# Graph attention: weighted rows in a tile of their own, carried counts taken from the destinations, the carried row read ahead of the copy, and two quads' logits in one PSUM bank

## The chip, the cores and the metric

The kernel runs on one core of a Trainium2 chip. The metric is the device time of one execution in microseconds (us), lower being better; it is stated as the median of several runs. PE is the tensor engine (PEld its weight loads), DVE the vector engine, ACT the scalar engine, POOL the GpSimd engine, and SP the engine that here only issues DMAs.

## What is computed

A residual layer of graph attention over 12,500 nodes of 128 values and 200,000 edges, sorted by destination, with 64 values per edge and 4 heads of 32:

```python
h = jnp.maximum(_layernorm(x, axis=-1), 0.0)
# _L0_gnn_ref(h, (src, dst), edge_attr_64, W_node, W_edge, a):
h = (node_features @ W_node.T).reshape(num_nodes, H, HD)
e = (edge_features @ W_edge.T).reshape(num_edges, H, HD)
att = jnp.sum(jnp.concatenate([h[src], h[tgt], e], axis=-1) * a, axis=-1)
att = jnp.where(att > 0, att, 0.2 * att)
m = jnp.maximum(jax.ops.segment_max(att, tgt, num_segments=num_nodes), 0.0)
ex = jnp.exp(att - m[tgt])
deg = jax.ops.segment_sum(ones, tgt, num_segments=num_nodes)
denom = segment_sum(ex, tgt) + (num_edges - deg)[:, None] * jnp.exp(-m)
w = ex / denom[tgt]
h_prime = segment_sum(w[:, :, None] * h[src], tgt)
# result: x + h_prime
```

## The kernel before

**Tiling.** Edges are cut into 392 groups of 511, each held as 4 chunks of 128 lanes (J = 4); lane 0 of a group is free for a row carried over from the group before, since a destination's edges can run across the boundary. Four groups are a quad (98 quads), and 2 to 4 quads are a super (28 of them), the unit of the softmax. A group's destinations lie within a window of 96 nodes (WIN).

**Prologue.** x is loaded, normalized and multiplied with the weights, and one row of 137 values per node goes to a table in HBM: 4 heads of 32 values and a one (132), a count (R_CNT), and 4 source logits (R_SRC). For the first four quads POOL gathers raw rows of x instead, which need no table (64 gathers from the start on). `indexed` derives the per-group tables from the destinations: the first node of each window (`base`), the lane's slot in the window, `is_last` (the lane's destination is the group's last one), and `cont` and `thru` (the group goes on with the destination before; it holds only that one).

**Main loop.** The order is written out by hand: `together` takes steps in turn from generators, so that in program order a group of `sums(q)`, a group of `all_logits` of a later quad and a step of `softmax(s)` alternate. Each engine runs its own instructions in that order, and waits on semaphores that other engines and DMAs raise.

- `fetch(q + 2)`, called when the logits of quad q open, issues the edge features and destinations (L283, L285), the windows (one TensorLoad of a register per group, L458), four small DMAs for target logits (`pw`, L468) and four for x (`xw`, L470) on SP, and 16 indirect gathers on POOL (L137), one for each chunk of 128 rows. The gathered rows go to `ga`, a ring of eight quads.
- `logits(q, i)` compares destinations (DVE, L500) and multiplies on PE (L505, L508) into `lg`. `flush` adds the pieces up (L520) and the source logits from `ga` (L522) into `U`.
- `softmax(s)` turns U over (L548), takes the slope (ACT L550, DVE L553), scans for the maximum over each destination (L557, L582, L584), and leaves in PSUM the exponentials `ex`, with the factors `facs` of the carried row and the maxima `xs` copied out (L607, L612).
- `sums(q)` writes the maxima over the source logits in `ga` (ACT, L680), multiplies the gathered values by `ex` in place (DVE, L687), builds the marks `hot` (DVE, L691) and sums the rows on PE: three matmuls for chunks 1 to 3 (L696), and a stop matmul for chunk 0 (L639), which waits for the carried row. `complete` runs one group late: it multiplies the carried row out of the PSUM `acc` of the group before (DVE, L634), copies the carried count (ACT, L638, one element), issues the stop matmul, and copies `acc` out to `pt` (ACT, L640). The matmuls are in float32 and appear as two each in the profile.
- After the last group of a quad, `divide` (L708 to L722) makes the result, and SP writes it with one DMA per group (L724), each after a register load of its own (L458).

The carried row of a group thus passes from PE (L639) over ACT (L640), DVE (L634) and ACT (L638) back to PE: L634 is placed behind L640, which reads the same `acc`. A slot of the ring `ga` is free once L639 of its group has read it.

## Time and profile before

| what | before |
|---|---|
| median of 3 runs | 2578.58 us (2570.87 to 2586.93) |
| profiled execution, its own time | 2600.19 us |
| its span | 2598.4 us |
| mean granted clock of PE | 0.536 of full speed |
| PE / PEld / DVE / ACT / POOL busy | 54 / 48 / 53 / 16 / 58% |
| HBM traffic | 114 GB/s over the span |
| stage of the gathers from the table | about 294 to 2473 us |

The profile is one execution on the chip, so sums over its instructions are to be held against its own 2600.19 us. A line number such as L639 is that of the kernel's source. An idle time is followed by what ended it; "issue" means that nothing in the profile held the engine, and "remote" that the event which ended the wait is not in the record.

### The profile page before, as it was taken

What the parts mean: (1) busy time and instruction counts of PE and PEld (TensorE: products, weight loads), DVE (VectorE), ACT (ScalarE), POOL (GpSimd) and SP (SyncE); (2) the same over time, 40 slices, a digit from 0 to 9 for tenths busy, and PEclk for the clock granted to TensorE, in tenths of its full rate; (3) what the DMA queues carried; (4) which work ended last, traced back from release to release, by engine and by line L of the source; (5) the groups of instructions that cost most, each with busy time, mean ns of one, the idle gap of its engine ahead of it and who ended that gap; (6) DMA issues with size and microseconds to landing.
All of it is one profiled execution on the core that took longest, in us unless ns stands there. A gap on an engine that the chain in (4) does not pass through costs nothing. (4 is left out here: it accounts for less than half of the span.)

```text
span 2598.4 us, 29393 instructions
## 1 busy us (share of the span) xinstructions
PE 1405.4 (54%) x7275; PEld 1256.7 (48%) x7275; DVE 1367.0 (53%) x3291; ACT 421.7 (16%) x1806; POOL 1508.0 (58%) x1609
## 2 busy tenths in 40 slices
PE   2442665555555555556555555655555555545485
PEld 1331655545545445445445544545544554444375
DVE  2441465555555545555554554654554554555486
ACT  1431411111111111111111111111111111111122
POOL 7235256666666666666666666666666666666603
PEclk9975655555555555555555555555555555555555
DMA  4342455544544454554455445454544544434430
GB/s 150 102 126 53 108 136 124 127 116 118 128 123 113 115 142 107 127 125 117 119 124 124 116 119 123 120 125 117 125 115 118 125 121 116 121 97 112 103 92 17
DMA packets 214495, 299.12 MB, mean 115 GB/s; under 512 B 86121, under 2 KB 162153, under 8 KB 204914
## 3 DMA queue, kind: packets, MB, share of 16 engines
q1 hardware_dynamic: 162512, 184.97, 26.6%
q0 software_dynamic: 50112, 109.65, 19.3%
q10 hardware_dynamic: 1698, 2.58, 0.3%
q8 instruction: 61, 1.00, 0.2%
q14 instruction: 112, 0.92, 0.1%
HBM read 270.49 MB, written 26.52 MB: 114 GB/s over the span
## 5 line engine op out<-in xcount | busy, mean ns | idle before, releaser
L137 POOL DMA_INDIRECT ga<-table,srci x1502 | 1426.7, 950 | 963.2 <-issue 406.0
L696 PE MATMUL acc<-ga,hot 128*97 128x137 f32 x2352 | 649.6, 448 | 341.3 <-ACT ga L680 225.1
L696 PEld LDWEIGHTS acc<-ga,hot 128*97 128x97 f32 x2352 | 518.2, 279 | 366.1 <-ACT ga L680 229.2
L634 DVE TENSOR_TENSOR ga<-acc,facs 1x132 f32<-1x132 f32 x391 | 115.9, 296 | 625.9 <-ACT pt L640 502.1
L639 PE MATMUL acc<-ga,hot 128*97 128x137 f32 x784 | 267.4, 444 | 289.0 <-ACT ga L638 215.5
L508 PE MATMUL lg<-wblk,ea 128*128 128x8 f32 x1568 | 410.5, 360 | 0.0
L508 PEld LDWEIGHTS lg<-wblk,ea 128*128 128x128 f32 x1568 | 383.3, 310 | 0.0
L505 PEld LDWEIGHTS <-at 96*128 96x128 bf16 x1568 | 219.7, 167 | 298.7 <-DVE at L500 115.0
L639 PEld LDWEIGHTS acc<-ga,hot 128*97 128x97 f32 x784 | 190.3, 279 | 320.3 <-ACT ga L638 235.8
L640 ACT COPY pt<-acc 97x137 f32<-97x137 f32 x392 | 107.4, 274 | 1431.8 <-remote 850.5
L505 PE MATMUL lg<-pw,at 96*128 96x12 bf16 x1568 | 170.7, 182 | 239.1 <-DVE at L500 101.2
L687 DVE TENSOR_TENSOR ga<-ga,ex_ps 128x528 f32<-128x528 f32 x392 | 270.0, 689 | 8.4 <-remote 8.0
L500 DVE TENSOR_TENSOR at<-const_ps,db 96x512 bf16<-96x512 f32 x392 | 267.1, 683 | 9.0 <-DMA db<-in_dst_dram 3.2
L691 DVE TENSOR_TENSOR hot<-const_ps,slot 128x384 f32<-128x384 f32 x384 | 209.4, 545 | 0.0
L520 DVE TENSOR_REDUCE st<-lg 128x64 f32<-128x192 f32 x98 | 35.0, 358 | 139.1 <-remote 109.7
L638 ACT COPY ga<-acc 1x1 f32<-1x1 f32 x391 | 59.9, 153 | 228.8 <-DVE ga L634 114.1
L375 PE MATMUL row_ps<-wcat,hT 128*128 128x137 f32 x198 | 40.3, 354 | 79.9 <-DVE hT L367 32.0
L600 PE MATMUL ex_ps<-ident,ex 64*128 64x64 f32 (+2 forms) x112 | 18.6, 315 | 115.6 <-ACT ex L589 49.7
L375 PEld LDWEIGHTS row_ps<-wcat,hT 128*128 128x128 f32 x198 | 34.0, 246 | 86.1 <-issue 46.0
L553 DVE TENSOR_TENSOR t_ps<-t_ps,low 64x511 f32<-64x511 f32 (+2 forms) x28 | 19.2, 687 | 104.4 <-issue 60.2
L137 POOL DMA_INDIRECT ga<-in_x_dram,srci x64 | 60.6, 947 | 20.9 <-issue 19.2
L600 PEld LDWEIGHTS ex_ps<-ident,ex 64*128 64x128 f32 (+2 forms) x112 | 13.8, 208 | 118.3 <-ACT ex L589 51.1
(131 smaller groups left out, 1131.1 us busy)
## 6 DMA issues: line engine op xcount, KB each, us to landing
db<-in_dst_dram SPq DMA_DIRECT2D x98, 768.0 KB
ea<-in_edge_t_dram SPq DMA_DIRECT2D x98, 512.0 KB
ga<-table,srci POOLq DMA_INDIRECT x1502
xw<-in_x_dram SPq DMA_DIRECT2D x392, 48.0 KB
out_dram<-res SPq DMA_DIRECT2D x392, 48.0 KB
pw<-side SPq DMA_DIRECT2D x392, 2.2 KB
table<-row SPq DMA_DIRECT2D x9, 616.5 KB
xt<-in_x_dram SPq DMA_DIRECT2D x9, 576.0 KB
```

Source lines behind the costliest of these rows:

```text
L137: nc.gpsimd.indirect_dma_start(out=ga[:, i, j, 0:width], out_offset=None, in_=rows, in_offset=bass.IndirectOffsetOnAxis(ap=srci[:, g0 + i, ...
L375: nc.tensor.matmul(row_ps[:, t, :ROW], hT[:, t, :], wcat, start=True, stop=True)
L500: nc.vector.tensor_tensor(at[:, i, :], node_ps[0:WIN, g0 + i:g0 + i + 1].to_broadcast([WIN, GE]), db[:, i, :], op=OP.is_equal)
L505: nc.tensor.matmul(lg[:, i, j].rearrange("p k h -> p (k h)"), at[:, i, j * P:(j + 1) * P], sw, start=i + j == 0, stop=False, skip_group_ch ...
L508: nc.tensor.matmul(lg[:, i, 2 * w:2 * w + 2, 0, :], ea[:, i, w, :], wblk, start=False, stop=True, skip_group_check=True)
L634: nc.vector.tensor_tensor(ga[0:1, i, 0, 0:H * HW].rearrange("p (h w) -> p h w", w=HW), before[WIN:WIN + 1, 0:H * HW].rearrange("p (h w) -> ...
L638: nc.scalar.copy(ga[0:1, i, 0, R_CNT:R_CNT + 1], before[WIN:WIN + 1, R_CNT:R_CNT + 1])
L639: nc.tensor.matmul(acc, hot[:, i, 0, :], ga[:, i, 0, :], start=False, stop=True)
L640: nc.scalar.copy(pt[:, i, :], acc)
L687: nc.vector.tensor_tensor(val, val, heads(ex)[:, :, :, g - s0].unsqueeze(3).to_broadcast([P, J, H, HW]), op=OP.mult)
L691: nc.vector.tensor_tensor(hot[:, i, :, 0:WIN], lane_ps.unsqueeze(1).to_broadcast([P, J, WIN]), slot[:, g, :].unsqueeze(2).to_broadcast([P, ...
L696: nc.tensor.matmul(acc, hot[:, i, j, :], ga[:, i, j, :], start=j == 1, stop=False)
```

## The change

- The product of gathered rows and exponentials goes to a new tile `gw` (two groups per buffer, two buffers) rather than back to `ga`. The maxima, with a leading column of ones that takes the place of the count, are copied into it once per pair of groups. The ring slot is thereby free once the multiply has read it.
- The counts carried into each group are computed once, in `indexed`: a matmul of ones with `is_last` (four, accumulated) and a scan over the groups into `came`. The per-group copy L638 goes, and so does the column of ones for the raw quads.
- The carried row is multiplied out of `acc` before `acc` is copied to `pt`; the copy and the exponential behind it move to a function `copied`, issued after the next group's stop matmul, and `divide` comes one `complete` later.
- The logits of two quads share one PSUM tile, and `flush` comes after the first group of the next quad's logits.
- The slope is applied to U in SBUF by one DVE operation; L550 and L553 go. `facs` is copied on one partition by DVE.
- The registers of a quad's windows are loaded by one multi-register load.
- The marks of the last two quads are made one quad ahead each, `hot` has two buffers rather than three, and a check at the end shares tiles with the softmax.

```diff
@@ -114,6 +114,9 @@
     base = consts.tile([1, G], I32, name="base")
     cont = consts.tile([1, G], F32, name="cont")
     thru = consts.tile([1, G], F32, name="thru")
+    came = consts.tile([1, G + 1], F32, name="came")
     flag = consts.tile([1, 1], I32, name="flag")
     quads = blocks(G, QG)
@@ -265,7 +268,6 @@
             nc.scalar.copy(
                 rows[:, :, 0:H * HW].rearrange("p t (h w) -> p t h w", w=HW)[:, :, :, HD],
                 ones[:, 0:1].unsqueeze(2).to_broadcast([P, m * J, H]))
-            nc.scalar.copy(rows[:, :, R_CNT], ones[:, 0:m * J])
             yield
@@ -325,6 +327,15 @@
                                         wide_ps[1].unsqueeze(2).to_broadcast([P, G, J]),
                                         op=OP.is_equal)
                 yield
+                ones_b = index.tile([P, 1], BF16, name="ones_b")
+                nc.vector.memset(ones_b, 1.0)
+                own_ps = wide_ps[0][0:1, :]
+                for j in range(J):
+                    nc.tensor.matmul(own_ps, ones_b, is_last[:, :, j], start=j == 0, stop=j == J - 1)
+                nc.vector.memset(came[:, 0:1], 0.0)
+                yield
+                nc.vector.tensor_tensor_scan(came[:, 1:G + 1], thru, own_ps, initial=0.0,
+                                             op0=OP.mult, op1=OP.add)
                 nc.vector.tensor_scalar(slot[0:1, :, 0], cont, -1.0, None, op0=OP.add)
@@ -444,8 +455,14 @@
         const_ps = ps.tile([P, WIN + G + QG * H], F32, name="const_ps")
         lane_ps, node_ps = const_ps[:, 0:WIN], const_ps[:, WIN:WIN + G]
         share_ps = const_ps[0:WIN, WIN + G:].rearrange("p (g h) -> p g h", h=H)
+        lg_all = ps.tile([P, 2, QG, J, PIECES, H], F32, name="lg")
         nc.vector.tensor_copy(lane_ps, lane)
         nc.vector.tensor_copy(node_ps, node_at)
+        xs_all = consts.tile([P, 2, J, 1 + H, SBG], F32, name="xs_all")
+        nc.vector.memset(xs_all[:, :, :, 0, :], 1.0)
         tops = consts.tile([1, H, len(supers) + 1], F32, name="tops")
         nc.vector.memset(tops, 0.0)
@@ -454,16 +471,18 @@
             g0 = quads[q0][0]
             return g0, quads[q0 + m - 1][0] + quads[q0 + m - 1][1] - g0
-        def window(g):
-            return nc.values_load(
-                base[0:1, g:g + 1], engines=[mybir.EngineType.SP], min_val=0, max_val=N - 1,
-                skip_runtime_bounds_check_because="a destination, which is a node")
+        def windows(q, lo=0, hi=QG):
+            g0, m = quads[q]
+            g0, m = g0 + lo, min(hi, m) - lo
+            return nc.values_load_multi_w_load_instructions(
+                base[0:1, g0:g0 + m], engines=[mybir.EngineType.SP], min_val=0, max_val=N - 1,
+                skip_runtime_bounds_check_because="a destination, which is a node")[1]
         def fetch_windows(q):
             g0, m = quads[q]
             pw = PW[q] = load.tile([WIN, QG, SIDE], BF16, name="pw")
             xw = XW[q] = work.tile([WIN, QG, D], F32, name="xw", bufs=8)
-            at = [window(g0 + i) for i in range(m)]
+            at = windows(q)
             for i in range(m):
                 nc.sync.dma_start(pw[:, i, :], side[bass.ds(at[i], WIN), :])
             for i in range(m):
@@ -488,7 +507,7 @@
             if q + 2 < nq:
                 fetch(q + 2)
             AT[q] = work.tile([WIN, QG, GE], BF16, name="at")
-            LG[q] = ps.tile([P, QG, J, PIECES, H], F32, name="lg")
+            LG[q] = lg_all[:, q % 2]
         def logits(q, i):
@@ -543,14 +562,14 @@
             same, same_next = kp[:R, 1:GE], kp[:R, 2:GE + 1]
             flush()
             u = U.pop(s)
+            nc.vector.scalar_tensor_tensor(u[:, :, :R], u[:, :, :R], SLOPE, u[:, :, :R],
+                                           op0=OP.mult, op1=OP.max)
             t_ps = ps.tile([SBG * H, GE], F32, name="t_ps")
             for j in range(J):
                 nc.tensor.transpose(t_ps[:R, j * P:(j + 1) * P], u[:, j, :R], ident)
             low = turned.tile([P, NE], F32, name="low")
-            nc.scalar.mul(low[:R], t_ps[:R, 1:GE], SLOPE)
             yield
             att = t_ps[:R, 1:GE]
-            nc.vector.tensor_tensor(att, att, low[:R], op=OP.max)
             run = turned.tile([SBG * H, GE], F32, name="run")
             nc.vector.memset(run[:R, 0:1], 0.0)
             run_e = run[:R, 1:GE]
@@ -583,7 +602,7 @@
             top = att
             nc.vector.tensor_tensor_scan(top[:, ::-1], same_next[:, ::-1], att[:, ::-1],
                                          initial=0.0, op0=OP.mult, op1=OP.max)
-            ex = turned.tile([SBG * H, GE], F32, name="ex")
+            ex = turned.tile([P, GE], F32, name="ex")
             nc.vector.memset(ex[:R, 0:1], 0.0)
             nc.vector.tensor_tensor(ex[:R, 1:GE], low[:R], top, op=OP.subtract)
             nc.scalar.activation(ex[:R, 1:GE], ex[:R, 1:GE], AF.Exp)
@@ -604,49 +623,55 @@
             fac_ps = other[:, 0:R]
             nc.tensor.matmul(fac_ps, ones[:R, :], diag[:R, :R], start=True, stop=True)
             facs = turned.tile([P, SBG * H], F32, name="facs", bufs=2)
-            nc.scalar.copy(facs[:, :R], fac_ps)
+            nc.vector.tensor_copy(facs[WIN:WIN + 1, :R], fac_ps[WIN:WIN + 1, :])
             top_ps = other[:, 512 - J * SBG * H:].rearrange("p (j r) -> p j r", j=J)[:, :, 0:R]
             for j in range(J):
                 nc.tensor.transpose(top_ps[:, j, :], run[:R, j * P:(j + 1) * P], ident[:R, :R])
-            xs = turned.tile([P, J, SBG * H], F32, name="xs", bufs=2)
-            nc.scalar.copy(xs[:, :, 0:R], top_ps)
+            xs = xs_all[:, s % 2]
+            nc.scalar.copy(xs[:, :, 1:, 0:m], top_ps.rearrange("p j (h g) -> p j h g", h=H))
+            nc.scalar.copy(xs[0:1, 0, 0, 0:m], came[:, g0:g0 + m])
             XS[s] = ex_ps[:, 0:J * SBG * H].rearrange("p (j r) -> p j r", j=J), xs, facs
             yield
-        begun = []
+        begun, divisions = [], []
         state = {}
         def complete():
-            division = state.pop("division", None)
+            due = [d for d in divisions if d[0] >= nq - 2 or d[-1] == 1]
+            divisions[:] = [d[:-1] + (1,) for d in divisions if d not in due]
+            full = state.pop("full", None)
             if begun:
                 complete_group(*begun.pop())
-            if division:
-                divide(*division)
-
-        def complete_group(q, i, ga, hot, pt, acc, fc):
-            g0, m = quads[q]
-            g = g0 + i
-            if g:
+            if full:
+                copied(*full)
+            for d in due:
+                divide(*d[:-1])
+        def complete_group(q, i, gw, hot, pt, acc, fc):
+            if quads[q][0] + i:
                 before = state["before"]
                 nc.vector.tensor_tensor(
-                    ga[0:1, i, 0, 0:H * HW].rearrange("p (h w) -> p h w", w=HW),
+                    gw[0:1, 0, 0:H * HW].rearrange("p (h w) -> p h w", w=HW),
                     before[WIN:WIN + 1, 0:H * HW].rearrange("p (h w) -> p h w", w=HW),
                     fc.unsqueeze(2).to_broadcast([1, H, HW]), op=OP.mult)
-                nc.scalar.copy(ga[0:1, i, 0, R_CNT:R_CNT + 1], before[WIN:WIN + 1, R_CNT:R_CNT + 1])
-            nc.tensor.matmul(acc, hot[:, i, 0, :], ga[:, i, 0, :], start=False, stop=True)
+            nc.tensor.matmul(acc, hot[:, i, 0, :], gw[:, 0, :], start=False, stop=True)
+            state["before"] = acc
+            state["full"] = q, i, pt, acc
+        def copied(q, i, pt, acc):
             nc.scalar.copy(pt[:, i, :], acc)
-            state["before"] = acc
             part = 1 if q == nq - 1 else 2 if q == nq - 2 else QG
-            if (i + 1) % part == 0 or i == m - 1:
+            if (i + 1) % part == 0 or i == quads[q][1] - 1:
                 lo = i - i % part
                 den = work.tile([WIN, QG, H], F32, name="den")
                 nc.scalar.activation(den[:, lo:i + 1, :], pt[0:WIN, lo:i + 1, R_SRC:R_SRC + H],
                                      AF.Exp, scale=-1.0)
-                state["division"] = q, pt, den, lo, i + 1
+                divisions.append((q, pt, den, lo, i + 1, 2))
@@ -656,7 +681,7 @@
         def marks(q):
             g0, m = quads[q]
-            hot = work.tile([P, QG, J, WIN + 1], F32, name="hot", bufs=3)
+            hot = work.tile([P, QG, J, WIN + 1], F32, name="hot")
             nc.scalar.copy(hot[:, :m, :, WIN], is_last[:, g0:g0 + m, :])
             if q >= nq - FREE:
                 for i in range(m):
@@ -677,15 +702,21 @@
             pt = work.tile([WIN + 1, QG, ROW], F32, name="pt", bufs=3)
             hot = HOT.pop(q) if q in HOT else marks(q)
             for i in range(m):
-                nc.scalar.copy(ga[:, i, :, R_SRC:R_SRC + H], heads(xs)[:, :, :, g0 - s0 + i])
-            for i in range(m):
                 g = g0 + i
-                if q == nq - 1 - FREE and i == 1:
-                    for k in range(FREE):
-                        HOT[nq - FREE + k] = marks(nq - FREE + k)
-                val = ga[:, i, :, 0:H * HW].rearrange("p j (h w) -> p j h w", w=HW)
+                if i == 1 and nq > q + 1 >= nq - FREE:
+                    HOT[q + 1] = marks(q + 1)
+                if i % 2 == 0:
+                    gw2 = work.tile([P, 2, J, ROW], F32, name="gw")
+                    n = min(2, m - i)
+                    nc.scalar.copy(
+                        gw2[:, 0:n, :, R_CNT:R_SRC + H],
+                        xs[:, :, :, g - s0:g - s0 + n].rearrange("p j h g -> p g j h"))
+                gw = gw2[:, i % 2]
+                by_head = lambda t: t[:, :, 0:H * HW].rearrange("p j (h w) -> p j h w", w=HW)
                 nc.vector.tensor_tensor(
-                    val, val, heads(ex)[:, :, :, g - s0].unsqueeze(3).to_broadcast([P, J, H, HW]),
+                    by_head(gw), by_head(ga[:, i]),
+                    heads(ex)[:, :, :, g - s0].unsqueeze(3).to_broadcast([P, J, H, HW]),
                     op=OP.mult)
                 if q < nq - FREE:
                     nc.vector.tensor_tensor(
@@ -693,9 +724,9 @@
                         slot[:, g, :].unsqueeze(2).to_broadcast([P, J, WIN]), op=OP.is_equal)
                 acc = ps.tile([P, 512], F32, name="acc", bufs=3)[0:WIN + 1, 0:ROW]
                 for j in range(1, J):
-                    nc.tensor.matmul(acc, hot[:, i, j, :], ga[:, i, j, :], start=j == 1, stop=False)
+                    nc.tensor.matmul(acc, hot[:, i, j, :], gw[:, j, :], start=j == 1, stop=False)
                 complete()
-                begun.append((q, i, ga, hot, pt, acc, fc[:, :, g - s0]))
+                begun.append((q, i, gw, hot, pt, acc, fc[:, :, g - s0]))
                 yield
         def divide(q, pt, den, lo, hi):
@@ -720,13 +751,16 @@
                 share_ps[:, :n, :].unsqueeze(3).to_broadcast([WIN, n, H, HD]), op=OP.mult)
             add = nc.gpsimd if nq - 1 > q >= nq - 1 - FREE else nc.vector
             add.tensor_tensor(res[:, :n, :], res[:, :n, :], xw, op=OP.add)
+            at = windows(q, lo, hi)
             for i in range(n):
-                nc.sync.dma_start(out[bass.ds(window(quads[q][0] + lo + i), WIN), :], res[:, i, :])
+                nc.sync.dma_start(out[bass.ds(at[i], WIN), :], res[:, i, :])
         def all_logits(q):
+            open_logits(q)
+            logits(q, 0)
+            yield
             flush()
-            open_logits(q)
-            for i in range(QG):
+            for i in range(1, QG):
                 logits(q, i)
                 yield
             state["logits"] = q
...
@@ -810,11 +843,12 @@
                     together(all_logits(a))
                 if not s:
                     complete()
+                    complete()
                     together(*late(3))
             flush()
             together(sums(nq - 1))
-            complete()
-            complete()
+            for _ in range(3):
+                complete()
             together(check_steps)
             redo = nc.values_load(flag[0:1, 0:1], min_val=0, max_val=1)
```

More of the change, by code (lines that the diff above doesn't have):

```diff
@@ L764, in checked @@
             for k, (g0, n) in enumerate(blocks(G, P)):
-                rows = turned.tile([P, NE + 1], I32, name="rows")
+                rows = turned.tile([P, GE], F32, name="ex").bitcast(I32)
                 nc.scalar.dma_start(rows[:n], dst_rows[g0:g0 + n, 0:NE + 1])
-                yield
                 falls = turned.tile([P, NE], F32, name="low")
```

## The prediction

> **What bounds the kernel now.** I read the page's busy shares first, then the windows, the waits, and the timeline of one pause.
>
> ```profile
> PE 1405.4 (54%) x7275; PEld 1256.7 (48%) x7275; DVE 1367.0 (53%) x3291; ACT 421.7 (16%) x1806; POOL 1508.0 (58%) x1609
> ```
> No engine is full. The windows compare the main stage with the tail, where no gathers are left to issue:
> ```profile
> 294.00:2473.00 2179.00, 1210.89 (x6244) 1085.94 (x6241) 1165.88 (x2632) 293.78 (x1418) 1366.26 (x1438) 0.50 0.49 119
> 2475.00:2550.00 75.00, 62.90 (x335) 58.18 (x336) 64.02 (x147) 16.61 (x78) 8.27 (x16) 0.50 0.29 76
> ```
> PE is 56% busy while gathers run (1210.89 of 2179) and 84% without them, at the same granted clock, 0.50. So PE, DVE and ACT are held up where gathers run. POOL's timeline has 1438 gathers there, start to start 1.25 us (0.95 + 0.30): 1793 us. The rest, 386 us, is pauses: I count 157 of over 0.7 us, 2.4 us each beyond the usual 0.30 (374 us), after stretches of 4, 8 or 12 gathers, 9.2 on average (2.3 groups). The waits name both sides:
> ```profile
> ACT pt L640 <- remote: 850.5, 102, 11.9
> DVE ga L634 <- ACT pt L640: 502.1, 141, 11.3
> POOL ga L137 <- remote: 245.4, 100, 3.3
> ACT pt L640 <- PE acc L639: 231.3, 164, 4.3
> PEld acc L639 <- ACT ga L638: 235.8, 55, 11.4
> POOL ga L137 <- PE acc L639: 146.5, 46, 15.2
> ```
> POOL waits for L639, the matmul that frees a ring slot (slots last eight quads). L639 waits for the carried row through PE, ACT (L640), DVE (L634), ACT (L638), PE. One pause in the timeline of all engines:
> ```profile
> 1900.88 0.66 PE L639 MATMUL acc<-ga,hot 128*97 128x137 f32 x2
> 1901.92 0.57 PE L508 MATMUL lg<-wblk,ea 128*128 128x8 f32 x2
> ...
> 1904.85 4.61 SPq L468 DMA_DIRECT2D pw<-side  x4
> 1905.85 0.94 POOL L137 DMA_INDIRECT ga<-table,srci  x1 [0.30 <-issue]
> 1909.34 0.27 ACT L640 COPY pt<-acc 97x137 f32<-97x137 f32 x1 [9.36 <-remote]
> ...
> 1909.58 0.94 POOL L137 DMA_INDIRECT ga<-table,srci  x1 [2.78 <-remote]
> ...
> 1909.65 0.29 DVE L634 TENSOR_TENSOR ga<-acc,facs 1x132 f32<-1x132 f32 x1 [8.05 <-ACT pt L640]
> ...
> 1909.89 1.69 PE L696 MATMUL acc<-ga,hot 128*97 128x137 f32 x6 [7.39 <-ACT ga L680]
> ```
> L639 ends at 1901.5, yet L640, which needs it, starts at 1909.34, 2.5 us after POOL's last gather. A signal raised in mid-stretch reaches its waiter only when POOL has stopped; POOL itself waits for the same signal. Early in a stretch signals pass at once. The prologue, which has no ring to wait for, shows the same: under 64 gathers back to back, DVE's L188 starts come 1.4 us apart for instructions of 0.29 us, and ACT's L376 sits 16 to 23 us. The cause of this slowness no view shows; I call it the jam. Its price is one pause per stretch, and **the number of groups that get through per stretch sets the main stage**: four gathers (5.0 us) plus a share of one pause (2.4/2.3 = 1.0 us) makes 6.0 us per group, against 6.06 measured (2179 us for 359.5 groups).
>
> **The change part by part.**
>
> *Carry and copy.* L638 goes (391 x 153 ns = 60 us of ACT), the counts come from a table made in the prologue, and the carry reads PSUM ahead of the pt copy. The loop from one stop matmul to the next becomes PE, DVE, PE: two crossings between engines instead of four. Outside a jam this hides behind PE: within the burst around 1899, L639 starts come 2.92 us apart (1897.96, 1900.88), and the old hops, 0.27 + 0.30 + 0.15 us, lie beside L505 to L696. Inside a jam every crossing is what waits. Floor: no gain, if what is late next (L505 on DVE's at, 115.0 us of waits, or the gw copy) jams as well. Ceiling: the whole 374 us. The nearest row is one stretch: with one more group through, 3.3 instead of 2.3, there are 359.5/3.3 = 109 pauses instead of 157, 48 x 2.4 = 115 us less; with half a group more, 67; with two more, 174. I take 107, near one group, because two of four crossings go but PE's own 2.92 us remain.
>
> *Fewer signals.* Counted over both instruction lists, instructions that raise a semaphore fall from 10463 to 8465 (PE 2250 to 1398, ACT 1803 to 1031). Worth 0 if the jam is a fixed delay (pauses after 4 and after 8 gathers average 2.4 us alike), up to 19% of 374 = 71 us if signals share one path. I take 0: the pauses do not grow with the work behind them.
>
> *Weighted rows in gw.* The multiply keeps its 128x528 and 0.69 us; only its target changes. ACT's four L680 copies per quad (216 ns) become two: 0.4 us per quad of a 16% engine, nothing. POOL now waits for DVE's multiply instead of L639: three groups earlier in the ring, once. It is no running gain, as a slot must still be consumed for each one filled. In the burst above the multiply of two groups on ends before L639 of this one, so its signal lies undelivered just the same: 0 here, but see the slower rival.
>
> *Softmax.* L550 (0.59 us) and L553 (0.69) go; one operation on 128x256 comes, nearest to L520's 0.36 us. 28 x 0.92 = 26 us off a chain that POOL covers in most supers; about 8 at the ends are less covered: -7 (0 to -26). facs on DVE: 28 x about 0.1 us, hidden.
>
> *Two quads' logits in a bank.* DVE's reduce of a quad now waits for the next quad's first logits on PE, about 1.1 us after a stop. Behind it on DVE stand U, at, the multiply and hot. From the stop: 1.1 + 0.36 + 0.27 + 0.69 (at) = 2.4 us, inside PE's 2.92; 0. Uncovered it would be 98 x 1.1 = 108 us.
>
> *Windows.* One multi-register load for four on SP (TensorLoad 785 to 201). SP's pw issues take 4.61 us in the jam, but they prefetch two quads ahead; 0 (to -10).
>
> *Ends.* Prologue: four matmuls on 392 columns and a scan of 392 on one partition (L557's 511 take 1.21 us): about 3 us, up to 10 if jammed. Tail: the hops shorten, about -4. Together -1.
>
> **Two rules against the trace.** The Trainium skill, "Perfetto Trace Analysis", Identifying the Most-Contended Engine, says that the engine with the highest occupancy is the bottleneck and is to be optimized first. That is POOL, 58%, and the change takes none of its gathers away: by the rule 0 us. The row says POOL stands idle 963.2 us, 374 of it in these pauses, so a shorter consumer loop can pay: 107. The same page, Optimization Strategy, says that the same gap repeating can mean too few buffers. By that, slots freed three groups earlier would end the pauses: -374. The row against it: pauses end with signals that were long due, and the gathered rows are some 41 gathers ahead of DVE's L522, so more room only shifts the ring.
>
> **Sum** against the profiled execution, 2600.2 us (span 2598.4): 2600.2 - 107 - 7 - 1 = 2485. The median of the runs is 2578.58, 0.9917 of it: 2465 us.
>
> **Rivals.**
> 1. *Nothing moves*: the jam lets through the same 2.3 groups whatever the loop, since all signals come in one burst. For: pause lengths are near constant. Against: half of the wait chain is ACT's. 2578 less 8 = 2570.
> 2. *Slower*: POOL's release now lies behind DVE. If the multiply has not run when POOL stops, the pause gains carry 0.30 + at 0.69 + multiply 0.69 = 1.7 us, during which PE does 0.6 of a group: 359.5/2.9 = 124 pauses x 4.1 = 508 us against 374, +134: 2711. It decides once DVE's in-order queue stands at the carry (line 657) with the needed multiply behind it in most pauses; half of them gives +67, 2645. For: DVE's carry already waits longest (502.1 us). Against: the trace above, where the multiply is ahead.
> 3. *Pauses vanish*: POOL runs through, -374 and the small terms: 2600 - 382 = 2218, times 0.9917: 2200. For: PE at 84% in the tail needs 4.0 us per group, less than POOL's 5.0. Against: the prologue, where unbroken gathers starve everyone.
>
> **How the numbers follow.** Forecast 0.49, its own range 2390 to 2530 (from 174 to 50 us saved); nothing 0.17; slower 0.25; vanishing pauses 0.09. A measurement of this kernel can tell about 1% from no change. The range 2310 to 2650 takes in the forecast, the nothing case, half of the slower case and part of the way to the floor. Faster 0.57, same 0.17, slower 0.26.
>
> **What would show it.** Right: about 110 POOL pauses of 2.4 us, more stretches of 12 and 16 gathers, gathers still 1.25 us apart, the wait of DVE's carry now on PE and under 400 us. Wrong: pauses as many as before (rival 1), pauses near 4 us ended by DVE's multiply (rival 2), or POOL near 65% busy with few pauses (rival 3). A gather spacing other than 1.25 us would break the whole sum.

## The result, and the profile after

The changed kernel takes 2828.45 us (median of 4 runs, 2819.46 to 2830.68) against 2575.08 us before (4 runs): a ratio of 1.0969, with a 95% interval of 1.0923 to 1.1015. It is slower by 9.7%. The profiled execution took 2819.46 us, with a span of 2817.6 us, against 2600.19 and 2598.4 before: 219 us more. (Between the medians it is 253 us; the execution that was profiled before is slower than its median.)

The page's busy shares (section 1) show hardly any work added; ACT does a quarter less, and every share falls because the span grew:

```profile
PE 1413.5 (50%) x7279; PEld 1233.6 (44%) x7279; DVE 1370.6 (49%) x3323; ACT 324.5 (12%) x1187; POOL 1505.0 (53%) x1609
```

The windows, main stage first, then the tail without gathers (columns: stretch, its length, busy time and instructions of PE, PEld, DVE, ACT, POOL, then clock, DMA share, GB/s):

```profile
293.00:2672.00 2379.00, 1214.91 (x6230) 1060.28 (x6230) 1161.61 (x2641) 203.21 (x847) 1363.01 (x1438) 0.51 0.43 109
2674.00:2749.00 75.00, 56.15 (x297) 50.72 (x297) 62.30 (x144) 11.13 (x44) 0.00 (x0) 0.50 0.31 79
```

The main stage grew from 2178 to 2379 us, by 201, for the same 1438 gathers. They still come 1.25 us apart. POOL's timeline gives the rest: 101 pauses of over 0.7 us instead of 157, but 577 us beyond the usual 0.30 in sum instead of 374, that is 5.7 us each instead of 2.4. The 203 us more of pauses are the growth of the stage. The tail grew by 20 us (125 to 146 from the last gather to the end). POOL now finishes up to three groups ahead of where it did; by the prediction's 4.0 us of PE for a group that would leave an estimated 12 us more of work to the tail, but no run isolates that.

The waits (engine and line that waited, what released it, us in sum, times, longest) show where the release moved to:

```profile
ACT pt L666 <- DVE gw L657: 1517.2, 259, 17.8
DVE gw L657 <- remote: 823.3, 110, 13.9
PEld acc L661 <- DVE gw L657: 610.1, 85, 12.8
...
POOL ga L140 <- DVE gw L717: 561.8, 94, 9.9
...
DVE col L599 <- remote: 114.0, 22, 7.0
```

DVE's carry (L657) has taken the place of ACT's copy as the one that waits for PE's late signal, and POOL is now released by DVE's multiply (L717) instead of by PE: 92 of the 101 pauses end with it. One stretch in the timeline of all engines (the carry needs L661's sum, and `at` is the comparison that PE's L524 needs):

```profile
1933.96 0.66 PE L661 MATMUL acc<-gw,hot 128*97 128x137 f32 x2
...
1936.17 0.68 DVE L519 TENSOR_TENSOR at<-const_ps,db 96x512 bf16<-96x512 f32 x1
...
1936.77 0.69 DVE L717 TENSOR_TENSOR gw<-ga,ex_ps 128x528 f32<-128x528 f32 x1
...
1936.91 0.22 PE L524 MATMUL lg<-pw,at 96*128 96x12 bf16 x2 [2.28 <-issue]
...
1937.38 0.55 DVE L722 TENSOR_TENSOR hot<-const_ps,slot 128x384 f32<-128x384 f32 x1
...
1945.09 0.94 POOL L140 DMA_INDIRECT ga<-table,srci  x1 [0.30 <-issue]
...
1949.08 0.30 DVE L657 TENSOR_TENSOR gw<-acc,facs 1x132 f32<-1x132 f32 x1 [11.15 <-remote]
1949.40 0.69 DVE L519 TENSOR_TENSOR at<-const_ps,db 96x512 bf16<-96x512 f32 x1
...
1949.43 0.77 PE L661 MATMUL acc<-gw,hot 128*97 128x137 f32 x2 [9.70 <-DVE gw L657]
1950.01 0.69 DVE L717 TENSOR_TENSOR gw<-ga,ex_ps 128x528 f32<-128x528 f32 x1
...
1950.97 0.94 POOL L140 DMA_INDIRECT ga<-table,srci  x1 [4.94 <-DVE gw L717]
```

PE's stop matmul ends at 1934.62, and the carry that needs it starts at 1949.08. In between DVE's signals are on time: `at` (L519) ends at 1936.85 and PE's L524 starts at 1936.91. POOL stops at 1946.03, because the multiply of the next group stands in DVE's queue behind the late carry. After PE's signal arrives, POOL waits for carry, `at` and multiply, and restarts at 1950.97: 1.89 us after the carry's start, where before it was 0.24 us after L640's.

This holds for both traces as a whole, from 320 us on, wherever the waiting engine had been idle for 0.2 us or more. Signals of DVE and ACT pass at once: after, PE's weight load of L524 starts 0.05 us behind L519 in all 157 cases, and that of L661 0.05 us behind L657 in all 108. Before, DVE's L634 starts 0.03 us behind ACT's L640 (187 cases), and ACT's L638 0.03 us behind L634 (197). PE's signal alone comes late: L640 starts more than 2 us behind L639 in 31% of 388 cases before, and L657 more than 2 us behind L661 in 61% of 179 after.

The carry is not the only thing that stands late in DVE's queue. Once in most supers POOL stops at this:

```profile
510.22 0.37 PE L596 MATMUL ex_ps<-ones,into 1*64 1x1 f32 x2
...
517.32 0.95 POOL L140 DMA_INDIRECT ga<-table,srci  x1 [0.30 <-issue]
519.89 0.15 DVE L599 COPY col<-ex_ps 64x1 f32<-64x1 f32 x1 [6.25 <-issue]
520.14 1.28 DVE L601 TENSOR_TENSOR_SCAN t_ps<-kp,col,t_ps 64x511 f32<-64x511 f32 x1
...
521.46 1.22 DVE L603 TENSOR_TENSOR_SCAN t_ps<-kp,t_ps 64x511 f32<-64x511 f32 x1
...
526.11 0.70 DVE L717 TENSOR_TENSOR gw<-ga,ex_ps 128x528 f32<-128x528 f32 x1
...
527.09 0.94 POOL L140 DMA_INDIRECT ga<-table,srci  x1 [8.82 <-DVE gw L717]
```

PE's L596 ends at 510.59, and the softmax's copy that needs it (L599) starts at 519.89. The multiply that POOL waits for stands behind the rest of the softmax, and POOL restarts 7.20 us after L599's start. The pauses sort as follows, by what stands on DVE between the late signal and the multiply (us beyond the usual 0.30):

| between the late signal and POOL's restart | pauses | us each | us in sum |
|---|---|---|---|
| carry, `at`, multiply (1.89 us) | 39 | 4.5 | 176 |
| carry, `at`, the opening of a softmax with the reduce of the logits, multiply (4.25 us) | 16 | 6.9 | 110 |
| the softmax from L599 on, multiply (7.2 us) | 22 | 8.9 | 195 |
| other | 24 | 4.0 | 96 |

### The profile page after: what moved, and what is told of

It is laid out like the page before. It is cut to its first block, busy times and chain, and to the rows that moved or that the text cites. A ratio compares the mean times of both kernels' runs of the same rounds, so it can differ in the third digit from the quotient of the medians.

```text
span 2817.6 us, 26972 instructions
## 1 busy us (share of the span) xinstructions
PE 1413.5 (50%) x7279; PEld 1233.6 (44%) x7279; DVE 1370.6 (49%) x3323; ACT 324.5 (12%) x1187; POOL 1505.0 (53%) x1609
## 4 chain that ended last, share of the span: by engine, by line
another core or an unknown queue 30%; DVE 28%; PE 11%; issue 9%; POOL 5%; DMA 1%; ACT 1%; SPq 0%; DVEq 0%; POOLq 0%
PE acc L727 5%; DVE at L519 5%; POOL ga L140 5%; DVE gw L717 5%; DVE hot L722 4%; DVE gw L657 3%; PE lg L527 2%; PE acc L661 2%; DVE res L753 2%; DVE res L749 2%; DVE t_ps L601 1%; DVE t_ps L603 1%; DVE U L541 1%; DVE den L744 1%
## 5 line engine op out<-in xcount | busy, mean ns | idle before, releaser
L727 PE MATMUL acc<-gw,hot 128*97 128x137 f32 x2352 | 640.4, 443 | 67.2 <-DVE hot L722 21.2
L661 PE MATMUL acc<-gw,hot 128*97 128x137 f32 x784 | 267.5, 444 | 661.5 <-DVE gw L657 578.6
L657 DVE TENSOR_TENSOR gw<-acc,facs 1x132 f32<-1x132 f32 x391 | 115.8, 296 | 922.2 <-remote 823.3
L727 PEld LDWEIGHTS acc<-gw,hot 128*97 128x97 f32 x2352 | 512.5, 276 | 98.5 <-issue 53.0
L661 PEld LDWEIGHTS acc<-gw,hot 128*97 128x97 f32 x784 | 184.8, 274 | 702.5 <-DVE gw L657 610.1
L527 PE MATMUL lg<-wblk,ea 128*128 128x8 f32 x1568 | 404.8, 356 | 0.0
L527 PEld LDWEIGHTS lg<-wblk,ea 128*128 128x128 f32 x1568 | 377.5, 306 | 0.0
L524 PEld LDWEIGHTS <-at 96*128 96x128 bf16 x1568 | 210.3, 164 | 296.4 <-issue 159.8
L524 PE MATMUL lg<-pw,at 96*128 96x12 bf16 x1568 | 168.7, 180 | 223.0 <-issue 133.2
L519 DVE TENSOR_TENSOR at<-const_ps,db 96x512 bf16<-96x512 f32 x392 | 267.5, 683 | 14.1 <-DMA db<-in_dst_dram 7.4
L717 DVE TENSOR_TENSOR gw<-ga,ex_ps 128x528 f32<-128x528 f32 x392 | 270.7, 691 | 1.3
L539 DVE TENSOR_REDUCE st<-lg 128x64 f32<-128x192 f32 x98 | 35.1, 358 | 96.9 <-remote 47.2
L689 POOL TENSOR_SCALAR hot<-lane,slot 128x96 f32<-128x96 f32 x32 | 17.1, 555 | 105.2 <-ACT hot L685 94.1
L749 DVE TENSOR_TENSOR res<-pt,const_ps 96x512 f32<-96x512 f32 (+2 forms) x102 | 67.5, 662 | 6.1 <-DMA out_dram<-res 1.8
```

The costliest lines, as they stand in the source:

```text
L519: nc.vector.tensor_tensor(at[:, i, :], node_ps[0:WIN, g0 + i:g0 + i + 1].to_broadcast([WIN, GE]), db[:, i, :], op=OP.is_equal)
L524: nc.tensor.matmul(lg[:, i, j].rearrange("p k h -> p (k h)"), at[:, i, j * P:(j + 1) * P], sw, start=i + j == 0, stop=False, skip_group_ch ...
L527: nc.tensor.matmul(lg[:, i, 2 * w:2 * w + 2, 0, :], ea[:, i, w, :], wblk, start=False, stop=True, skip_group_check=True)
L657: nc.vector.tensor_tensor(gw[0:1, 0, 0:H * HW].rearrange("p (h w) -> p h w", w=HW), before[WIN:WIN + 1, 0:H * HW].rearrange("p (h w) -> p ...
L661: nc.tensor.matmul(acc, hot[:, i, 0, :], gw[:, 0, :], start=False, stop=True)
L717: nc.vector.tensor_tensor(by_head(gw), by_head(ga[:, i]), heads(ex)[:, :, :, g - s0].unsqueeze(3).to_broadcast([P, J, H, HW]), op=OP.mult)
```

## The experiments

Ratios are to the kernel before on the same chip, with 95% intervals. The chips differ between groups of runs (e1 to e4; e5 to e8; e9 to e11; e12 to e15; e16 to e18): the kernel before took 2598, 2572, 2602, 2595 and 2572 us on them. A comparison across groups is therefore good to about 1%, and where it matters the times stand beside the ratios. "Pauses" are those of POOL over 0.7 us in the main stage (the last 1438 gathers) of the profiled execution, and their sum is what exceeds the normal idle time between gathers.

**e1: the product back in the ring.** In the changed kernel:

```diff
-                    gw2 = work.tile([P, 2, J, ROW], F32, name="gw")
                     n = min(2, m - i)
+                    gw2 = ga[:, i:i + n]
```

> The changed kernel with the product written back into the ring ga instead of gw, so that a gather waits for PE's stop matmul again; everything else of the change stays. Theory A (the loss comes from the slot's release being moved behind DVE's in-order queue, which at the end of each pause first works off the carry, 0.30 us, at, 0.69 us, and the multiply, 0.69 us): the restart after the first late carry is again 0.24 us instead of 1.9 to 4.25, POOL's pauses add up to about 370 us instead of 578, time 2560 to 2640 us. Rival B (the order of carry and copy, the shared logits bank or the deferred divide cost the time): it stays near 2830 us. Rival C (the parts besides gw are a gain): clearly below 2550 us.

Measured: 2677.28 us, 1.0291 (1.0246 to 1.0335); 145 pauses, 444 us. About 6.6% of the kernel's time goes with `gw` (1.0969/1.0291 = 1.066; by the times, 2828.45 and 2677.28 us on two chips, 5.6%), so theory A holds for the largest part, but not for all: a loss of 2.9% stays. That `gw` has only two buffers is not the reason: in the changed kernel DVE stands idle before the multiply for 1.3 us in sum (last number):

```profile
L717 DVE TENSOR_TENSOR gw<-ga,ex_ps 128x528 f32<-128x528 f32 x392 | 270.7, 691 | 1.3
```

The waits of e1 point to a second place:

```profile
DVE ga L657 <- remote: 353.8, 55, 11.1
...
DVE st L539 <- remote: 218.7, 29, 11.3
...
POOL ga L140 <- PE acc L661: 133.0, 25, 7.7
```

DVE's reduce of the logits (L539) waits 218.7 us, where L520 before waited 109.7.

**e2: `gw` alone.** The kernel before, with the product written to a tile of its own. To make room, `hot` has two buffers and the marks of the last two quads are made one quad ahead each, as in the change (e1 keeps both). Part of the edit:

```diff
+                if i % 2 == 0:
+                    gw2 = work.tile([P, 2, J, ROW], F32, name="gw")
...
+                    by_head(gw), by_head(ga[:, i]), heads(ex)...
```

> The kernel before with only the tile gw of the change (product of the gathered rows written to gw, the source maxima and a one copied there; hot with two buffers, and the marks of the last two quads made one quad ahead each, as gw needs the room). Theory A: POOL waits for DVE's multiply, pauses fewer and longer, time 2750 to 2850 us. Rival B (the cost is in the other parts): 2560 to 2610 us.

Measured: 2750.56 us, 1.0583 (1.0544 to 1.0621); 147 pauses, 525 us; POOL waits 489.3 us for the multiply. The one part alone costs 5.8%, close to what e1 showed from the other side.

**e3: the multiply right behind the carry.** In the changed kernel, DVE's order becomes carry, multiply of the next group, divide, `at`, inside a quad; the first multiply of a quad keeps its place. Part of the edit (`then` is the next group's multiply with its copy into `gw`):

```diff
             if begun:
                 complete_group(*begun.pop())
+            then()
             if full:
                 copied(*full)
...
-                complete()
+                complete(lambda: weigh(i + 1) if i + 1 < m else None)
```

> The changed kernel with one change in DVE's order: the multiply of the next group stands right behind the carry, ahead of at and of the divide. Theory A: from the late carry to POOL's restart 0.30 + 0.69 + about 0.27 = 1.3 us instead of 1.9 (4.25 where a divide lies between); 65 pauses hold such a carry, so 65 x 1.3 = about 85 us less: 2700 to 2780 us. If POOL's longer stretches as such are the cost, not the chain behind the carry, it stays at 2820 to 2840 us.

Measured: 2945.18 us, 1.1321 (1.1271 to 1.1371): a miss in the wrong direction. The timeline shows why:

```profile
1929.61 0.94 POOL L140 DMA_INDIRECT ga<-table,srci  x1 [0.30 <-issue]
1933.70 0.30 DVE L658 TENSOR_TENSOR gw<-acc,facs 1x132 f32<-1x132 f32 x1 [9.99 <-remote]
...
1935.01 0.68 DVE L756 TENSOR_TENSOR res<-pt,const_ps 96x512 f32<-96x512 f32 x1
1935.73 0.69 DVE L760 TENSOR_TENSOR res<-res,xw 96x512 f32<-96x512 f32 x1
1936.34 0.68 DVE L519 TENSOR_TENSOR at<-const_ps,db 96x512 bf16<-96x512 f32 x1
1936.94 0.69 DVE L717 TENSOR_TENSOR gw<-ga,ex_ps 128x528 f32<-128x528 f32 x1
...
1937.90 0.94 POOL L140 DMA_INDIRECT ga<-table,srci  x1 [7.35 <-DVE gw L717]
```

The restart is 1.30 us behind the carry inside a quad, as expected, but POOL's stops moved to the turn between quads, where the first multiply still stands behind the divide (2.3 us) and `at`: 4.2 us from carry to restart, in 51 of 114 pauses. The divide had its place there in the changed kernel too, but few pauses fell on it. 63 stretches of e3 are of 16 gathers, one quad, and the pauses add up to 722 us. In e3 the stops settled where the chain behind the carry is longest.

**e8: e3 with the divide one group later**, away from that turn. Part of the edit:

```diff
-                divisions.append((q, pt, den, lo, i + 1, 2))
+                divisions.append((q, pt, den, lo, i + 1, 3))
```

> e3 (multiply right behind the carry) with the divide one group later, so that at the turn from one quad to the next no divide (2.36 us) stands between the late carry and the next quad's multiply. In e3 the stops of POOL all moved to that place (56 stretches of 16 gathers, restarts 4.2 us behind the carry). Theory A: restart 1.3 to 1.9 us behind the carry, about 90 such pauses, 90 x 2.2 = about 200 us less than e3: ratio 1.04 to 1.07, below the changed kernel's 1.097. If not the chain behind the carry but the longer stretches cost the time: ratio 1.10 to 1.14 as e3.

Measured: 2753.32 us, 1.0705 (1.066 to 1.0749), just above the expected band; 117 pauses, 520 us. In 79 of them POOL restarts 1.3 or 1.9 us behind the late carry; in some 20 a softmax still stands between. POOL's wait for the multiply fell from 716.2 us in e3 to

```profile
POOL ga L140 <- DVE gw L717: 509.1, 107, 8.3
```

Moving six DVE operations by one group is worth 5% of the time (1.0705/1.1321); stretches of 16 gathers are nearly as many as in e3 (60). So the chain behind the late carry costs the time, not the length of the stretches.

**e5: e1 with the reduce ahead of the next quad's first logits.**

```diff
         def all_logits(q):
+            flush()
             open_logits(q)
-            logits(q, 0)
-            yield
-            flush()
-            for i in range(1, QG):
+            for i in range(QG):
```

> e1 (product written back into the ring) with the reduce of a quad's logits back ahead of the next quad's first logits, as before; the two quads' logits still share a bank. Theory: e1's remaining loss of 2.9% is this reduce: placed behind the next quad's first logits it makes DVE's in-order queue wait for a fresh signal of PE once a quad (DVE st L539 waits 218.7 us in e1, L520 109.7 before), and PE's signals are the ones that come late. Then it goes back to the time before, within 1.5%: ratio 0.985 to 1.015. Rival (carry ahead of the copy, the deferred copy or the counts cost it): ratio stays 1.02 to 1.04.

Measured: 2618.59 us, 1.0189 (1.0144 to 1.0235); 137 pauses, 382 us. Outside both bands: by the ratios the reduce's place costs about 1% (1.0291/1.0189), a third of what the theory gave it; by the times, on two chips, 2.2%.

**e9: e5 with `acc` copied right behind its stop matmul.** The divide thereby also comes one group earlier.

```diff
             state["before"] = acc
-            state["full"] = q, i, pt, acc
+            copied(q, i, pt, acc)
```

> e5 (product in the ring, reduce ahead of the next logits) with acc copied to pt right behind its stop matmul again, so that DVE's carry waits for ACT's copy as before; the counts from the destinations, the shared bank, the softmax and the window loads of the change stay. If the order of carry and copy is the rest of the loss (e5 1.019): ratio 0.985 to 1.005. If it is one of the parts that stay: 1.01 to 1.03. If shortening the loop was a gain that something else ate up: above 1.03.

Measured: 2617.18 us, 1.0062 (1.0037 to 1.0086), just outside the expected band; 155 pauses, 375 us. By the ratios the order of carry and copy accounts for 1.3% (1.0189/1.0062); by the times of e5 and e9, on two chips, for nothing. e1 and e9 ran on chips on which the kernel before took nearly the same (2598 and 2602 us), and are 2.3% apart: that much the places of the reduce and of the copy cost together, and how it splits between them is open. What is left of the change in e9 (counts from the destinations, shared bank, softmax, window loads) costs 0.6% and gains nothing that shows.

**e4 and e6: are the loads on SP to blame?** In the timelines PE's signals often turn late when the edge loads of a quad start. e4 uses the first two quads' edges again; e6 also their windows, by the same lines in `fetch_windows`. The edit of e4:

```diff
         def fetch_edges(q):
+            if q > 1:
+                EA[q], DB[q] = EA[q - 2], DB[q - 2]
+                return
```

> The kernel before without the loads of edge features and destinations from the third quad on (the tiles of the first two quads are used again, so the logits are those of other edges). In both traces PE's signals turn late within a few us of the start of these two loads (1.28 MB per quad). If the loads together with the gathers bring on the jam: pauses mostly gone, 2200 to 2350 us. If the gathers alone do: 2500 to 2580 us.

> The kernel before with no loads on SP in the main loop but the destination rows of the softmax (edge features, destinations, target logits and x windows of the first two quads are used again), so that next to the gathers only the writes of the result are left. If the gathers alone make PE's signals late: ratio 0.98 to 1.02, pauses still about 150 of 2.4 us. If SP's small DMAs, which take 4.6 to 8.6 us in the jam, bring it on: pauses mostly gone, ratio under 0.93.

Measured: e4 2608.71 us, 1.0039 (1.0021 to 1.0057), above its 2500 to 2580 us only because the kernel before takes 2598 on that chip; e6 2613.91 us, 1.0161 (1.0107 to 1.0216). In e6 nothing is left beside the gathers but the result's writes and the softmax's destination rows, and the waits on late signals are there as before (118 pauses, 387 us in sum):

```profile
ACT pt L646 <- remote: 816.4, 91, 12.1
...
POOL ga L137 <- PE acc L645: 223.9, 40, 14.0
POOL ga L137 <- remote: 190.3, 76, 3.8
```

The loads coincide with the lateness and do not cause it: gathers, with the little that e6 leaves beside them, are enough. Why e6 is 1.6% slower stays open.

**e7 and e11: gathers further apart**, in the kernel before, by a memset on POOL behind each gather from the table; one element in e7, 128 x 512 in e11.

```diff
+                if q >= raw:
+                    nc.gpsimd.memset(spare, 0.0)
```

> The kernel before with one memset of a single element on POOL after every gather from the table: the gathers come some 0.1 to 0.4 us further apart. If signals are late because gathers are issued faster than they are worked off, a slower issue lets them through: pauses shrink by more than the spacing adds, ratio below 1. If any unbroken issue holds them up: pauses stay at 2.4 us each and the spacing is added in full, 1438 times its length (0.2 us: ratio 1.10).

> The kernel before with a memset of 128 x 512 on POOL after every gather from the table (a memset of one element fitted into the 0.30 us between two gathers and left them 1.25 us apart). Gathers come an estimated 0.2 to 0.5 us further apart. If only an issue rate of 1.25 us holds up PE's signals, POOL's pauses vanish and the ratio stays under 1.05. If any unbroken run of gathers does, pauses stay at 150 or so of 2.4 us and the spacing is added in full: ratio above 1.10.

In e7 the memset (0.09 us) fitted into the 0.30 us between gathers; they stayed 1.25 us apart, and the ratio is 1.0039 (1.0019 to 1.0058). It tells nothing on the rate. In e11 the memset took 0.54 us and the gathers came 1.65 us apart. That alone would add 0.40 x 1438 = 575 us; measured was 2696.93 us, 1.0361 (1.0326 to 1.0396), 95 us more. No pause was left at all, and ACT's copy (L644 there) waits for nothing but PE's own time:

```profile
  PE acc L643: 495.7, 288
  PE acc L700: 190.4, 103
  issue: 1.0, 1
```

The longest of these waits is 4.3 us, and no "remote" is among them, where before it was 850.5 us. The lateness belongs to gathers issued 1.25 us apart, not to gathers as such.

**e10: a ring of seven quads** in the changed kernel (QUADS = 7).

> The changed kernel with a ring of seven quads instead of eight. The change lets a slot go about three groups earlier; a ring shorter by four groups takes that lead away, and leaves the release behind DVE's queue. Theory A (what counts is the chain behind the late carry at each restart, not how far POOL may run ahead): ratio 1.085 to 1.11, as the changed kernel's 1.097. Rival (POOL running further ahead makes longer stretches and so longer stalls): ratio below 1.06.

Measured: 3059.47 us, 1.1753 (1.172 to 1.1786). This run doesn't answer its question: the hand-written order issues the gather of quad q + 7 beside the first group of sums(q), so that with seven slots rows are overwritten before they are summed, and sums come to wait for gathers of a later quad.

**e12 to e17: between 1.25 and 1.65 us**, and both kernels. The changed kernel has `xw` with seven buffers here, for room.

> The changed kernel with the memset of 128 x 512 on POOL after every gather from the table (1.65 us from gather to gather, at which e11 showed no late signals of PE; xw with seven buffers instead of eight, to make room). If the change costs time only through late signals (theory A: each restart of POOL waits for DVE's queue behind the late carry), nothing is left to lose here: ratio 1.02 to 1.04, as e11's 1.036. If parts of it cost PE or DVE time by themselves: ratio above 1.06.

> The kernel before with a memset of 128 x 240 after every gather from the table: by e7 (1 element 0.09 us) and e11 (512 elements 0.54 us) about 0.30 us, and 1.40 us from gather to gather. If signals pass at that rate, the main stage is 1438 x 1.40 = 2013 us instead of 2178: ratio 0.93 to 0.95. If gathers are worked off more slowly than 1.40 us, signals still come late and the pauses stay: ratio 1.00 to 1.09.

> The changed kernel with the memset of 128 x 240 (xw with seven buffers). If signals pass at 1.40 us: 0.93 to 0.95, as e13. If they are late at that rate: between 1.0 and the changed kernel's 1.10.

> The kernel before with a memset of 128 x 320: about 0.37 us, 1.47 us from gather to gather. If signals pass at that rate but not at 1.40: pauses gone, main stage 2114 us, ratio 0.97 to 0.98. If they pass at 1.40 too: the same 0.97 to 0.98, above e13. If they do not pass: above 1.0.

> The kernel before with a memset of 128 x 280 after every gather from the table: by e13 (240: 1.425 us from gather to gather) and e15 (320: 1.490 us) 1.457 us. If 7 pauses at 1.490 grow to 20 or fewer: main stage 1438 x 1.457 = 2095 us instead of 2152, ratio 0.925 to 0.945. If the rate at which signals turn late lies between: pauses come back as in e13 (78), ratio 0.95 to 0.99.

> The changed kernel with a memset of 128 x 320 after every gather from the table (xw with seven buffers). If the loss of the change is a matter of late signals alone: at 1.490 us within 1.5% of e15, ratio 0.945 to 0.965. If it costs by itself: above 0.98.

| gathers apart, us | before: ratio | pauses | changed: ratio | pauses |
|---|---|---|---|---|
| 1.25 | 1 | 157 | 1.0969 (1.0923 to 1.1015) | 101 |
| 1.42 | e13 0.993 (0.9911 to 0.9948) | 78 | e14 1.0184 (1.0127 to 1.0242) | 63 |
| 1.46 | e16 0.9521 (0.9479 to 0.9562) | 7 | | |
| 1.49 | e15 0.9497 (0.9478 to 0.9516) | 7 | e17 0.9591 (0.9562 to 0.9619) | 6 |
| 1.65 | e11 1.0361 (1.0326 to 1.0396) | 0 | e12 1.0459 (1.0436 to 1.0483) | 0 |

(At 1.65 us, where the regular idle time is 0.70 itself, pauses are those over 1.1 us.) Between 1.42 and 1.46 us the pauses go from 78 to 7. Late signals themselves thin out more slowly: ACT's copy waits for "remote" 767.4 us in e13, 126.5 in e16, 202.5 in e15 and not at all in e11. e16 has the 7 pauses that its lower band asked for, but came out at 0.952, not under 0.945: its profiled execution took 2427 us, its other three 2440 to 2457, against a kernel before that took 1% less on this chip than on e15's. e12 lies just above its band, and e13 just below the second of its bands. At 1.49 us the main stage is 2152 us, 1438 x 1.490 = 2143 of it gathers. POOL is then the bound, busy with gathers and memsets:

```profile
PE 1401.6 (57%) x7275; PEld 1252.2 (51%) x7275; DVE 1385.8 (56%) x3291; ACT 423.8 (17%) x1806; POOL 2079.0 (84%) x3111
```

e15 did better than its 0.97 to 0.98, and not by its main stage, which is only 26 us shorter than before. The stage begins 38 us earlier (257 instead of 295; why, no run isolates), and the tail behind the last gather is 71 us shorter (54 instead of 125). The waits show why the tail is short: in e15 DVE's sum of the source logits (L526, before L522) has caught up with POOL and waits for gathered rows, so that little is left to do when the last one lands. Before, it hardly ever did:

```profile
DVE U L526 <- DMA ga<-table,srci: 513.8, 65, 13.0
...
DVE U L522 <- DMA ga<-table,srci: 0.4, 1, 0.4
```

The changed kernel costs at most 1% against the kernel before with the same spacing (0.9591/0.9497 and 1.0459/1.0361; by the times 2466.14 against 2464.33 us and 2714.05 against 2696.93), not 9.7%. That fits a loss that comes nearly all through late signals. It doesn't prove it: with POOL as the bound, a cost on another engine can be hidden.

**e18: the prologue's raw gathers spaced too.** e15 without the condition `if q >= raw`.

> e15 with the 64 raw gathers of the prologue spaced as well: they end 64 x 0.24 = 15 us later, but POOL then waits 78 us for the node table in any case, and the node stage loses the stalls of 16 to 23 us that ACT shows there under the raw gathers. If these stalls are late signals too: 30 to 60 us below e15, ratio 0.925 to 0.94. If the prologue is held up by something else: 0.945 to 0.96.

Measured: 2393.08 us, 0.931 (0.9282 to 0.9337), the fastest here. ACT's copies of the node rows in the prologue, before (L376) in the timeline:

```profile
14.71 0.48 ACT L376 COPY row<-row_ps 128x411 f32<-128x411 f32 x1
...
33.05 0.50 ACT L376 COPY row<-row_ps 128x411 f32<-128x411 f32 x1 [16.34 <-remote]
...
58.27 0.50 ACT L376 COPY row<-row_ps 128x411 f32<-128x411 f32 x1 [18.57 <-issue]
```

and in e18 (L379):

```profile
18.09 0.50 ACT L379 COPY row<-row_ps 128x411 f32<-128x411 f32 x1 [1.00 <-PE row_ps L378]
...
21.00 0.48 ACT L379 COPY row<-row_ps 128x411 f32<-128x411 f32 x1
...
23.12 0.50 ACT L379 COPY row<-row_ps 128x411 f32<-128x411 f32 x1 [0.27 <-ACT hn L213]
```

They come 2 to 3 us apart instead of 18 to 25, and the first of the last 1438 gathers starts at 195 us, in e15 at 257, before at 295.

## Why the prediction was wrong

**Right:** what bounds the kernel (POOL's gathers plus pauses that end when a late signal comes), the gather spacing, and that fewer and longer stretches would follow. Rival 2 named the mechanism that decided: DVE's work between PE's signal and POOL's restart. That 109 pauses were forecast and 101 came is luck: the reason given was the shorter loop, and with it, but with the release put back, there are 145 (e1) or 137 (e5).

**The step that failed** is "the multiply of two groups on ends before L639 of this one, so its signal lies undelivered just the same: 0 here". It took the lateness for one of all engines. Both traces show DVE's signals to PE on time (0.05 us from the end of `at` to PE's load for its logits, in 95 of 95 cases before and 157 of 157 after) while PE's waits 14 us in the stretch shown. POOL had thus long used up the multiplies that were ahead, and stopped at one behind the stuck carry or the stuck softmax. The three groups of lead in the ring were used up once, as the prediction said; they bought nothing. What was put at 0 costs 5.8% alone (e2).

**The gain of 107 us failed by the same premise**, "Inside a jam every crossing is what waits". Of the loop's four crossings only PE's to ACT was late. The prediction's own lines have it: L640 ends at 1909.61, and L634, on another engine, starts at 1909.65. The crossings taken away had cost 0.03 us each, and the late one stayed, now from PE to DVE. With release and reduce put back, e5 has fewer pauses than e9 (137 against 155), but of 2.8 instead of 2.4 us: 382 us in sum against 375, so no gain. The price of a pause, 2.4 us, is not a constant.

**The sizes.** Rival 2 put the pause at 4.1 us and their sum at 508 us, for 2711 us. Measured: 5.7 us and 577 us. For the chain that it named, carry, `at` and multiply, it was near: 39 pauses of 4.5 us. What it left out is the softmax in the same queue: its opening with the reduce adds 2.36 us in 16 pauses, and in 22 others the softmax itself holds the late signal and 6.2 us of work stand before the multiply. These 38 pauses hold 305 of the 577 us. This is read from the trace; no run moves the softmax.

**The reduce in the shared bank** was costed at 0, inside PE's 2.92 us. That sum held for signals on time. It is one more wait of DVE for a fresh signal of PE each quad, and costs 1 to 2% (e5 against e1). **Carry ahead of the copy** comes out between no change and a loss of 1.3% (e9 against e5). In the order of before, one late signal of PE releases ACT and POOL together: 137 of the 157 pauses end 0.24 us behind a late copy. With the carry first, in e5, 48 pauses end 0.7 us and 27 end 0.2 us behind a late carry. **Fewer signals** were put at 0: no gain showed in e9, so nothing speaks against that step. The **softmax's** -7 and the **windows'** 0 cannot be told from e9's 0.6% loss.

**The two rules.** The Trainium skill's "Perfetto Trace Analysis", Identifying the Most-Contended Engine, takes POOL, as the busiest, for the bottleneck to work on first. e15 makes it busier, 84% instead of 58%, and takes 5% off the time. Its Optimization Strategy reads a repeating gap as a possible lack of buffers; the change gave the ring three groups more, and the gaps grew from 374 to 577 us.

**Open** is how gathers 1.25 us apart hold up PE's signals, and why those of DVE and ACT pass in the main stage. In the prologue, under the raw gathers, not only PE is slow: the four starts of L188 that come 1.4 us apart (20.36 to 24.61 us) and DVE's L198, 1.23 us behind L196, need nothing from PE. The same page (DMA Instruction, SWDGE) says that the profiler's end of such a gather is the end of descriptor generation, not of the transfer. The traces agree: by the order of the queue's packets, 32 for each gather, the last one ends 1.3 us (median) after POOL's instruction. That holds for the first gather of a stretch as for the twelfth, before and after the change, with at most 2.5 us in between, so a growing backlog of transfers is not the cause.

## What to carry to other kernels

When an engine is released by a signal that comes late, count everything that stands in an in-order queue between that signal and the release: moving the release from the engine that raises the late signal to one that must first work off its queue costs that queue at every stop. Count also what comes by only once in a while, such as a softmax step. Ask of each engine separately whether its signals are late; look for a pair of instructions on either side of the stall, already in the trace before the change. And if the busiest engine pauses over and over while all others wait for it, try to slow it: a spacing that just removes the pauses can be faster than full speed, here because the others keep up and less is left at the end.

## What the runs showed of the hardware that was not expected

- Beside indirect gathers of 128 rows, issued by POOL 1.25 us apart, PE's signals to ACT and DVE come 8 to 14 us late in the stretches shown, until 2.3 to 2.9 us after POOL stops (means before and after); signals of DVE and ACT pass in 0.03 to 0.05 us meanwhile. At 1.46 us 7 of 157 pauses are left, at 1.65 us no pause, and no "remote" wait in the main stage. It does not need the loads of the main loop (e6).
- A memset on POOL behind each gather took 0.09 us for one element, 0.31 for 128 x 240, 0.38 for 128 x 320 and 0.54 for 128 x 512; the first is hidden in the 0.30 us between gathers.
- 1502 such memsets of 128 x 320, work that the result does not need, took 5% off the time, and with 64 more in the prologue 7%.
